# Table scatters in four spaced pairs per batch, each released by a cast, and a first plan a quarter later, in a gated attention and mixture-of-experts layer

## The chip, the cores and the metric

The kernel runs on one core of a Trainium2 chip. The metric is device time in microseconds (us) of one execution; lower is better. One execution was also taken by the hardware profiler, and every view below is of that one.

## The reference

The layer takes eight batches of 512 tokens with 256 features. Attention comes first: sixteen heads of sixteen features over a context, with a mask, and a gated sum into x. Then a normalised x goes through eight experts, of which each token uses its best two:

```python
logits = x_flat @ router_w + router_b
probs = jax.nn.softmax(logits, axis=-1)
top_w, top_idx = jax.lax.top_k(probs, TOP_K)
comb = jnp.sum(top_w[..., None] * jax.nn.one_hot(top_idx, E, dtype=x.dtype), axis=1)
output = jnp.zeros_like(x_flat)
for e in range(E):
    h = jax.nn.gelu(x_flat @ expert_up[e].T, approximate=False)
    out_e = h @ expert_down[e].T
    output = output + comb[:, e:e + 1] * out_e
```

The result is `x + tanh(g_ffn) * output`. The kernel computes only the two chosen experts of each token.

## The kernel before

**Two kinds of work share the engines.** A loop of passes (`for b in range(-1, B)` in `attend_near`) does attention for batch b, prepares batch b+1 and finishes older ones. Each pass has four groups g, and each group three places n; a slot is written (g, n). `between` fills a table `plan[g, n]` of steps, and the loop runs them in that order. The other kind of work is the expert jobs.

**Jobs.** Tokens are sorted by expert in groups of 256 rows (a pair of 128-row halves; four late jobs have one half). A job fetches its rows by an indirect gather (`fetch`, `xg`), turns them on TensorE (`turn`, `x_ps`), does the up product in four steps (`ups`, `h_ps`, line 622), GELU on ScalarE, the down product in two (`downs`, `o_ps`, line 640), adds the weighted result to rows `y` gathered from the output (`fetch_y`, line 594), and scatters them back (line 646). `load` brings an expert's two weight matrices, 1024 KB each, on SP's queue; their pool has three buffers. There are 36 jobs in the main list.

**The table.** Where a token goes is known after routing. `place` (GpSimd, lines 440 to 460) counts each token's place in its expert's list, leaves it in `at` and casts it to integers in `place_i`. `enter(t)` then scatters 128 tokens' entries to the `table` in DRAM, once for each of the two chosen experts: two indirect DMAs on GpSimd's queue (line 464), four calls a batch, eight scatters. `count` of `plan(k)` (VectorE, lines 506 to 556) works out, once a part of the batches is placed, which expert and which table line each job of that part has. `list_rows(s)` reads a job's lines of the table back to SBUF (`listed`) on SP's queue (line 576). The table is one DRAM tensor, so a list read waits for the scatters issued before it, and a later scatter waits for a list read issued before it.

**Order.** The framework's scheduler may issue an instruction earlier than its place in the program when its operands are ready sooner; a pinned instruction (`keep_in_program_order`) stays behind the instruction that the program put before it on the same engine. [...]The steps of a batch's placing run one pass after its routing: `place` at slot (0, 2), and `enter` at (0, 2), (1, 0), (1, 1), (1, 2), or, in a pass whose batch completes a part (b = 4 for the first part, b = 7 for the second), all at (0, 2) with `counts` behind.

**First jobs in the loop.** `amid` names, for (pass, group), the job steps that run among attention's: `begin` (the first list reads, gathers and loads) in (4, 3), the first up product in (5, 1), and jobs 0 to 3 complete by the end of pass 7. `DONE = 4` is the first job of the tail.

**The tail.** After the loop, `compute(s, MAIN, DONE)` gives each job's steps, eleven for a pair in the middle: the gather for job s+2, the y gather of s-1, four up steps, the turn of s+1, two down steps of s-1, the list read of s+3, the load of s+2. After each step one entry of `queue` runs: the last batch's remaining attention steps (`rest`), then places and entries of batches 6 and 7 with empty entries (`wait`) between them, then the last plans.

Of the kernel before, what the change touches and what calls it, by code (L numbers as in the profile page):

```python
# [24 lines left out]
QT = S // P  # L25
# [38 lines left out]
def flamingo_layer(ctx: ExitStack, tc: tile.TileContext, a: dict, out: bass.AP):  # L64
    nc = tc.nc
# [82 lines left out]
    place_i = fixed([P, B * QT, 2], "place_i", I32)  # L148
# [145 lines left out]
    def shared(p2, small, bank):  # L294
# [72 lines left out]
        def finish(b):  # L367

            x2T = p2.tile([P, DC, S], F32, tag="xnT", name=f"x2T{b}", bufs=1)
            said = {}  # L370
# [58 lines left out]
            def place():  # L429

                both = said["both"].rearrange("p t e -> p (t e)")
                ps = bank(f"place_ps{b}")
                n = QT * E
                nc.tensor.matmul(ps[:, :n], lhsT=before, rhs=both, start=True, stop=True)
                nc.tensor.matmul(ps[:, n : 2 * n], lhsT=ones, rhs=both, start=True, stop=True)
                counts = small.tile([P, 2, QT, E], F32, tag="counts", name=f"counts{b}", bufs=2)
                nc.scalar.copy(counts.rearrange("p i t e -> p (i t e)"), ps[:, : 2 * n])
                place = t3("place")
                for t in range(QT):
                    nc.gpsimd.tensor_tensor(place[:, t, :], counts[:, 0, t, :], filled, ALU.add)  # L440
                    nc.gpsimd.tensor_tensor(filled, counts[:, 1, t, :], filled, ALU.add)
                mine = slice(b * QT, (b + 1) * QT)
                at = small.tile([P, QT, 2], F32, tag="at", name=f"at{b}", bufs=2)
                picked = said["picks"]
                nc.gpsimd.tensor_tensor(
                    picked, picked, place.unsqueeze(2).to_broadcast([P, QT, 2, E]), ALU.mult
                )
                for k in (4, 2, 1):
                    nc.gpsimd.tensor_tensor(
                        at.unsqueeze(3) if k == 1 else picked[..., :k], picked[..., :k], picked[..., k : 2 * k],  # L450
                        ALU.add,
                    )
                entry = entries[:, b % 2]
                nc.gpsimd.tensor_copy(
                    entry[:, :, :, :2], tokens_i[:, mine].unsqueeze(2).unsqueeze(3).to_broadcast([P, QT, 2, 2])
                )
                nc.gpsimd.tensor_scalar(
                    entry.bitcast(F32)[:, :, :, 2], said["top"][:, :, :2], tg[:, 1:2], None, ALU.mult
                )
                nc.gpsimd.tensor_copy(place_i[:, mine, :], at)  # L460

            def enter(t):
                for i in range(2):
                    nc.gpsimd.indirect_dma_start(  # L464
                        out=table_parts[2 * t + i][:, :],
                        out_offset=bass.IndirectOffsetOnAxis(ap=place_i[:, t, i : i + 1], axis=0),
                        in_=entries[:, b % 2, t % QT, i, :], in_offset=None,
                    )
# [225 lines left out]
    def attend_near(att):  # L694
# [245 lines left out]
        def begin():  # L940
# [6 lines left out]
                list_rows(s)  # L947

        amid = {
            (4, 3): [lambda: None, lambda: None, begin],  # L950
            (5, 0): [lambda: None, lambda: None, lambda: turn_rows(0)],
            (5, 1): [lambda: fetch(2), lambda: fetch_y(0)] + ups(0),
            (5, 2): downs(0)[:1] + [lambda: load(2)],
            (5, 3): downs(0)[1:] + [lambda: turn_rows(1)],
            (6, 0): [lambda: fetch(3), lambda: fetch_y(1)] + ups(1),
            (6, 1): downs(1)[:1] + [lambda: load(3)],
            (6, 2): downs(1)[1:],
            (6, 3): [lambda: turn_rows(2)],
            (7, 0): [lambda: fetch(4), lambda: fetch_y(2)] + ups(2),
            (7, 1): downs(2) + [lambda: load(4), lambda: turn_rows(3)],  # L960
            (7, 2): [lambda: fetch_y(3)] + ups(3),
            (7, 3): [lambda: list_rows(5), lambda: list_rows(6), lambda: fetch(5)] + downs(3)
            + [lambda: load(5), lambda: turn_rows(4)],
        }
        DONE = 4


        xnT, later = {}, deque()
# [8 lines left out]
        for b in range(-1, B):  # L977
# [6 lines left out]
            plan = between(*(n if 0 <= n < B else None for n in (b - 1, b + 2, b + 3)))  # L984
            for place, enter, counts in behind_route:
                plan[0, 2].append(place)
                if counts:
                    plan[0, 2] += enter + counts
                else:
                    for where, step in zip(((0, 2), (1, 0), (1, 1), (1, 2)), enter):  # L990
                        plan[where].append(step)
            for g in range(4):
                c, i = g // 2, g % 2
                if b >= 0:
# [17 lines left out]
        rest = [step for steps in between(B - 1, None, None).values() for step in steps]  # L1012
        wait = lambda: None
        (place, enter, _), (last, enter_last, counts) = later
        mixed = [step for pair in zip(rest, [place, *enter] + [wait] * len(rest)) for step in pair]
        spread = [step for one in enter_last for step in (one, wait, wait)]
        queue = deque([*mixed, wait, last, *spread, *counts])
        for s in range(DONE, MAIN):
            for step in compute(s, MAIN, DONE):
                step()  # L1020
# [330 lines left out]
```

## Time and profile before

| what | us |
|---|---|
| runs, median of 3 | 853.23 (847.31 to 854.47) |
| the profiled execution | 875.95 |
| its span | 874.2 |
| last table scatter of batch 7 issued at | 476.36 |
| first up product of the first job at | 277.65 |

Times in a view count from the start of the span. PE is TensorE's matmuls, PEld its weight loads, DVE is VectorE, ACT ScalarE, POOL GpSimd, and SP the queue that issues the plain DMAs. The page cuts the span into 40 slices of 21.9 us and gives each engine's busy share in tenths; PEclk is the clock granted to TensorE, in tenths of full speed. A row of a timeline has its start, its length, engine, line, operation and operands, a count, and in brackets the engine's idle time before it and what ended it. A wait row has who waited for whom, the total, the number of waits and the longest.

### The profile page before, as it was taken

Reading aid. Unit: us, or ns where it says so; the run is one execution under the profiler, and the core shown is the slowest. Engines: PE = TensorE matmul, PEld = TensorE weight load, DVE = VectorE, ACT = ScalarE, POOL = GpSimd, SP = SyncE. Lnnn points to the kernel's source line nnn. Section 1 sums busy time; section 2 is a strip of 40 time slices with the busy share of each in tenths; the row PEclk is TensorE's granted clock in tenths of the full one; section 3 lists DMA queues with packets and bytes.
Section 4 is the critical chain, followed back from the end, with each engine's and each line's share of the span. In section 5 each row is a group of like instructions: output and inputs, shape, how many; then the busy total and the mean of one; then the engine's idle time right before and its main releaser. Section 6 shows DMA issues by size and latency. Waiting matters only on the chain. (4 is left out here: it accounts for less than half of the span.)

```text
span 874.2 us, 11291 instructions
## 1 busy us (share of the span) xinstructions
PE 797.5 (91%) x4090; PEld 579.2 (66%) x4090; DVE 315.8 (36%) x945; ACT 260.3 (30%) x501; POOL 319.4 (37%) x431
## 2 busy tenths in 40 slices
PE   1798999898799989999999699999999999999992
PEld 0353444343445566676878588888898898989881
DVE  5366778484868355653232011111110110111110
ACT  0444464445264523444331112111111111111210
POOL 5111105141345225164545443534333433434331
PEclk9778999696989999999999899999999999999997
DMA  4600011101066221315454857565667676667611
GB/s 140 244 7 7 7 49 33 49 26 50 2 211 215 81 79 57 116 31 189 136 158 137 296 157 244 177 228 184 213 190 246 197 240 198 209 222 241 211 49 35
DMA packets 86630, 121.59 MB, mean 139 GB/s; under 512 B 15693, under 2 KB 70368, under 8 KB 86560
## 3 DMA queue, kind: packets, MB, share of 16 engines
q1 hardware_dynamic: 74400, 93.68, 32.1%
q0 software_dynamic: 12160, 27.04, 10.1%
q8 instruction: 36, 0.59, 0.3%
q14 instruction: 34, 0.28, 0.1%
HBM read 101.05 MB, written 20.17 MB: 139 GB/s over the span
## 5 line engine op out<-in xcount | busy, mean ns | idle before, releaser
L640 PE MATMUL o_ps<-down,hT 128*128 128x256 f32 x1088 | 245.0, 383 | 7.2 <-DVE y L643 6.7
L622 PE MATMUL h_ps<-xT,up 128*128 128x256 f32 (+1 forms) x1152 | 245.3, 370 | 5.8 <-DVE oT L871 2.6
L622 PEld LDWEIGHTS h_ps<-xT,up 128*128 128x128 f32 x1152 | 209.5, 191 | 35.8 <-DVE oT L871 3.0
L640 PEld LDWEIGHTS o_ps<-down,hT 128*128 128x128 f32 x1088 | 205.9, 192 | 40.1 <-DVE y L643 7.2
L626 ACT ACTIVATE hT<-h_ps 128x512 f32<-128x512 f32 (+1 forms) x144 | 81.5, 573 | 364.7 <-PE h_ps L622 316.0
L643 DVE SCALAR_TENSOR_TENSOR y<-o_ps,listed,y 128x256 f32<-128x256 f32 x68 | 32.8, 484 | 280.1 <-DMA y<-out,listed 149.5
L594 POOL DMA_INDIRECT y<-out,listed x68 | 66.1, 971 | 157.0 <-DMA out<-y,listed 125.5
L646 POOL DMA_INDIRECT out<-y,listed x68 | 68.7, 1010 | 105.6 <-DVE y L643 76.6
L845 ACT ACTIVATE n_pT<-w_ps 128x512 f32<-128x512 f32 x128 | 71.0, 599 | 82.7 <-PE w_ps L841 58.6
L816 DVE TENSOR_REDUCE tops<-t_ps 128x4 f32<-128x512 f32 x128 | 79.4, 681 | 39.2 <-PE t_ps L812 39.0
L594 POOL DMA_INDIRECT xg<-rows,listed x68 | 64.8, 954 | 42.6 <-DMA listed<-table 17.7
L841 PE MATMUL w_ps<-ql,n_km 32*128 32x512 f32 x256 | 74.7, 714 | 3.5 <-DVE tops L816 2.5
L464 POOL DMA_INDIRECT table<-entries,place_i x64 | 62.4, 975 | 25.9 <-issue 16.5
L612 DVE COPY xT<-x_ps 128x512 f32<-128x512 f32 (+1 forms) x36 | 23.6, 655 | 98.9 <-PE x_ps L610 92.9
L812 PE MATMUL t_ps<-n_k,n_q 32*128 32x256 f32 x512 | 50.9, 429 | 2.7 <-ACT n_pT L845 1.8
L799 POOL TENSOR_TENSOR x<-x,bo 128x1024 f32<-128x1024 f32 x8 | 19.0, 2372 | 78.6 <-ACT xn_a L341 78.6
L812 PEld LDWEIGHTS t_ps<-n_k,n_q 32*128 32x128 f32 x512 | 29.8, 196 | 26.1 <-issue 13.4
L792 PE MATMUL q_ps<-n_xnT,wqT 128*128 128x512 f32 x64 | 36.7, 705 | 7.0 <-ACT n_q L796 6.9
L863 DVE STREAM_TRANSPOSE raw<-n_av 128x512 f32<-128x512 f32 x32 | 22.8, 713 | 51.6 <-PE n_av L858 40.4
L841 PEld LDWEIGHTS w_ps<-ql,n_km 32*128 32x128 f32 x256 | 23.7, 204 | 24.2 <-DVE tops L816 16.3
L858 PE MATMUL n_av<-n_pT,nv 128*32 128x512 f32 x256 | 39.5, 676 | 0.0
L878 PE MATMUL proj_ps<-woT,oT 128*128 128x256 f32 x128 | 32.9, 392 | 4.8 <-DVE oT L871 4.8
(208 smaller groups left out, 563.8 us busy)
## 6 DMA issues: line engine op xcount, KB each, us to landing
up<-in_upT SPq DMA_DIRECT2D x36, 1024.0 KB
down<-in_downT SPq DMA_DIRECT2D x36, 1024.0 KB
x<-in_x SPq DMA_DIRECT2D x8, 512.0 KB
out<-x SPq DMA_DIRECT2D x8, 512.0 KB
rows<-xn_f SPq DMA_DIRECT2D x8, 512.0 KB
table<-none SPq DMA_DIRECT2D x1, 2288.0 KB
xg<-rows,listed POOLq DMA_INDIRECT x68
y<-out,listed POOLq DMA_INDIRECT x68
```

Of the source, the lines that this page charges most:

```text
L464: nc.gpsimd.indirect_dma_start(out=table_parts[2 * t + i][:, :], out_offset=bass.IndirectOffsetOnAxis(ap=place_i[:, t, i : i + 1], axis=0) ...
L594: nc.gpsimd.indirect_dma_start(out=dst, out_offset=None, in_=src[: seen[JOBS[s][0]], :], in_offset=bass.IndirectOffsetOnAxis(ap=listed[:, ...
L622: nc.tensor.matmul(ps[:, i, :n], lhsT=up[:, dc, (f + i) * P : (f + i + 1) * P], rhs=xT[:, dc, :n], start=(dc == 0), stop=(dc == DC - 1),)
L626: nc.scalar.activation(made[s][:, f : f + 2, :n], ps[:, :, :n], AF.Gelu)
L640: nc.tensor.matmul(ps, lhsT=hT[:, f, h * P : (h + 1) * P], rhs=down[:, f, :], start=(f == 0), stop=(f == FC - 1))
L646: nc.gpsimd.indirect_dma_start(out=out_parts[h][:, :], out_offset=bass.IndirectOffsetOnAxis(ap=listed[:, n, h, 0:1], axis=0), in_=y[:, h, ...
L792: nc.tensor.matmul(ps, lhsT=w["wqT"][:, dc, c * P : (c + 1) * P], rhs=xnT[b][:, dc, :], start=(dc == 0), stop=(dc == DC - 1),)
L812: nc.tensor.matmul(ps[j][:, u], lhsT=q[rows_j, c, t * P : (t + 1) * P], rhs=k[rows_j, c], start=True, stop=True)
L816: nc.vector.tensor_reduce(top[:, 2 * tp : 2 * tp + 2, :].rearrange("p t (i x) -> p t i x", i=2)[:, :, :, 32 * j], ps[j], AX.X, ALU.max,)
L841: nc.tensor.matmul(ps[j], lhsT=km[rows_j, c, i, :], rhs=lowered[b, c][rows_j, i, :], start=True, stop=True)
L845: nc.scalar.activation(pT[:, j, :], ps[j], AF.Exp)
L858: nc.tensor.matmul(av[32 * j : 32 * j + 32, :], lhsT=made[b][3][:, 8 * c + 2 * j + r, :], rhs=pT[:, j, :], start=True, stop=True,)
```

## The change

The cast of the places moves from the end of `place` (one on GpSimd for a batch) into `enter` (one on VectorE for each call, pinned in program order), so that each pair of scatters has to wait for a VectorE instruction at a fixed place. The slots of the four calls become (1, 1), (2, 0), (2, 2), (3, 1), for every batch, and `counts` goes to (1, 2). `begin` goes to (5, 0), the first up product to (5, 3); jobs 0 to 2 are complete by the end of the loop, and `DONE` is 3. In the tail `rest` runs first without gaps, then each placing and entering step is followed by four empty entries.

```diff
-                nc.gpsimd.tensor_copy(place_i[:, mine, :], at)
+                said["at"] = at
 
             def enter(t):
+
+                tc.keep_in_program_order(nc.vector.tensor_copy(place_i[:, t, :], said["at"][:, t % QT, :]))
                 for i in range(2):
                     nc.gpsimd.indirect_dma_start(
...
         amid = {
-            (4, 3): [lambda: None, lambda: None, begin],
-            (5, 0): [lambda: None, lambda: None, lambda: turn_rows(0)],
-            (5, 1): [lambda: fetch(2), lambda: fetch_y(0)] + ups(0),
-            (5, 2): downs(0)[:1] + [lambda: load(2)],
-            (5, 3): downs(0)[1:] + [lambda: turn_rows(1)],
-            (6, 0): [lambda: fetch(3), lambda: fetch_y(1)] + ups(1),
-            (6, 1): downs(1)[:1] + [lambda: load(3)],
-            (6, 2): downs(1)[1:],
-            (6, 3): [lambda: turn_rows(2)],
-            (7, 0): [lambda: fetch(4), lambda: fetch_y(2)] + ups(2),
-            (7, 1): downs(2) + [lambda: load(4), lambda: turn_rows(3)],
-            (7, 2): [lambda: fetch_y(3)] + ups(3),
-            (7, 3): [lambda: list_rows(5), lambda: list_rows(6), lambda: fetch(5)] + downs(3)
-            + [lambda: load(5), lambda: turn_rows(4)],
+            (5, 0): [lambda: None, begin],
+            (5, 2): [lambda: turn_rows(0)],
+            (5, 3): [lambda: fetch(2), lambda: fetch_y(0)] + ups(0),
+            (6, 0): downs(0)[:1] + [lambda: load(2)],
+            (6, 1): downs(0)[1:] + [lambda: turn_rows(1)],
+            (6, 2): [lambda: fetch(3), lambda: fetch_y(1)] + ups(1),
+            (6, 3): downs(1)[:1] + [lambda: load(3)],
+            (7, 0): downs(1)[1:] + [lambda: turn_rows(2)],
+            (7, 1): [lambda: fetch(4), lambda: fetch_y(2)] + ups(2),
+            (7, 2): downs(2)[:1] + [lambda: load(4)],
+            (7, 3): downs(2)[1:] + [lambda: turn_rows(3), lambda: list_rows(5)],
         }
-        DONE = 4
+        DONE = 3
...
                 plan[0, 2].append(place)
-                if counts:
-                    plan[0, 2] += enter + counts
-                else:
-                    for where, step in zip(((0, 2), (1, 0), (1, 1), (1, 2)), enter):
-                        plan[where].append(step)
+                plan[1, 2] += counts
+                for where, step in zip(((1, 1), (2, 0), (2, 2), (3, 1)), enter):
+                    plan[where].append(step)
...
-        mixed = [step for pair in zip(rest, [place, *enter] + [wait] * len(rest)) for step in pair]
-        spread = [step for one in enter_last for step in (one, wait, wait)]
-        queue = deque([*mixed, wait, last, *spread, *counts])
+        queue = deque([*rest, place, wait, wait])
+        for step in (*enter, last, *enter_last):
+            queue.extend([step] + [wait] * 4)
+        queue.extend(counts)
```

## The prediction

> **What bounds the kernel now.** I read the page's busy shares and slices first, then the timeline of the matmuls for where each batch begins, then busy time by batch, and last the waits and timelines around the idle stretches. The chain that ended last is no help: it holds only the last scatter.
>
> ```profile
> PE 797.5 (91%) x4090; PEld 579.2 (66%) x4090; DVE 315.8 (36%) x945; ACT 260.3 (30%) x501; POOL 319.4 (37%) x431
> PE   1798999898799989999999699999999999999992
> PEclk9778999696989999999999899999999999999997
> ```
>
> TensorE is the bound, so time can come only from its idle slices and from slices at a low granted clock. There are three places: slices 8 and 10 (clock digit 6), slice 11 (7 busy), slice 23 (6 busy). The same by stage, each line from a batch's first weights matmul to the next one's (columns: length, busy time with counts, granted clock, DMA share, GB/s):
>
> ```profile
> 96.25:130.37 34.12, 32.48 (x210) 16.08 (x209) 26.46 (x66) 19.80 (x41) 2.34 (x1) 1.00 0.11 36
> 130.37:175.03 44.66, 40.69 (x214) 18.92 (x213) 29.84 (x88) 20.59 (x43) 13.50 (x24) 0.82 0.13 41
> 175.03:219.28 44.25, 40.86 (x214) 18.81 (x213) 28.85 (x86) 20.29 (x43) 13.63 (x24) 0.81 0.12 38
> 219.28:261.28 42.00, 36.76 (x214) 17.06 (x214) 31.96 (x101) 20.41 (x43) 19.13 (x30) 0.90 0.30 102
> 261.28:311.87 50.59, 48.08 (x287) 28.98 (x286) 29.23 (x82) 23.53 (x46) 19.23 (x30) 1.00 0.47 154
> 311.87:359.27 47.40, 44.41 (x259) 28.69 (x258) 27.59 (x81) 17.54 (x31) 17.13 (x29) 0.93 0.29 89
> 359.27:410.66 51.39, 49.82 (x265) 34.89 (x264) 24.38 (x91) 21.57 (x37) 22.84 (x35) 1.00 0.29 95
> 484.86:508.24 23.38, 16.66 (x67) 14.06 (x68) 1.96 (x4) 2.39 (x4) 10.55 (x11) 0.85 0.69 238
> 508.24:858.50 350.26, 349.49 (x1726) 309.04 (x1724) 39.67 (x75) 58.02 (x104) 139.18 (x143) 1.00 0.61 200
> ```
>
> The first line is pass b=1: attention, no scatter, no expert job, 34.1 us. Passes 2 and 3 do the same matmuls and take 10 us more; the only new work is the placing and eight scatters on GpSimd (2.34 to 13.5 us). Around the end of pass 2's eight:
>
> ```profile
> 154.67 0.96 POOL L464 DMA_INDIRECT table<-entries,place_i  x1 [0.30 <-issue]
> ...
> 157.12 0.72 DVE L863 STREAM_TRANSPOSE raw<-n_av 128x512 f32<-128x512 f32 x1 [3.77 <-remote]
> ...
> 157.95 2.70 PE L792 MATMUL q_ps<-n_xnT,wqT 128*128 128x512 f32 x4 [3.67 <-ACT n_q L796]
> ```
>
> The last scatter's issue ends at 155.6; VectorE, ScalarE and TensorE all stand until 157.1 and go on together, with no named releaser. Pass 3 repeats it (last scatter 198.92 + 0.96, TensorE idle 1.95 us). After each the clock is 0.50 for some 17 us. What holds the engines is not shown; the end of the burst is what both have in common. Passes 5 to 7 also have eight back to back and no such stop.
>
> The tail (508 to 858) is full. Before it, 484.86 to 508.24 holds one job's matmuls and takes 23.4 us; these are the waits from 478 to 500, then the SP queue's over the span (total, times, longest):
>
> ```profile
> DVE y L643 <- DMA y<-out,listed: 18.9, 1, 18.9
> PE o_ps L640 <- DVE y L643: 6.7, 1, 6.7
> POOL y L594 <- DMA out<-y,listed: 6.4, 1, 6.4
> POOL xg L594 <- DMA listed<-table: 3.9, 1, 3.9
> ...
> SPq L576 <- DMA table<-entries,place_i: 29.5, 4, 20.8
> ```
>
> The chain reads backwards: SP sits up to 20.8 us at a list read until the last batch's scatters have landed (its next read goes at 478.90, the last scatter at 476.36); three jobs' weight loads then leave in one burst, GpSimd's gather waits for its list, the scatter of y leaves late, the next y gather later, and VectorE can't free the PSUM bank.
>
> [...]one n_o multiply at 225.47 took 2.42 us, against a mean of 0.49, beside the 2.34 us bias add on GpSimd.
>
> **The change, part by part.**
>
> *Spacing, passes 2 and 3.* Without the stop they would take b=1's 34.1 us: (44.66 − 34.12) + (44.25 − 34.12) = 20.7 us. Bounds: 0, if something else holds the engines, to −20.7. In the profiled execution I take −18.
>
> *Spacing, pass 4.* 42.0 − 34.1 = 7.9 us, but the 3.07 us gap at 225 [...]before any scatter, and the plan's VectorE work stays. I take −2 (0 to −5).
>
> *Casts.* 8 GpSimd casts of 0.19 us go; 32 VectorE casts come, priced by the nearest row, the index cast of 128x32 at 181 ns: 5.8 us, 24 of them (4.3 us) inside the passes, where VectorE is busy 26 to 32 us a pass. I take +1.5 (0 to +4.3); in the tail VectorE is nearly idle.
>
> *The wait that a cast adds.* VectorE stands at a pinned cast until GpSimd has `at`; behind it are the maxima and transposes that TensorE waits for. `at` was done at 189.45 in pass 3 and 236.0 in pass 4; the statistics after which the cast is pinned ran from about 193 and 241.8. The margin is 4 to 6 us, so 0; it would pay if gathers hold GpSimd longer. On GpSimd, gathers and y scatters now stand behind a pair that waits for its slot; y is needed half a job (7 us) later, which hides it.
>
> *First plan, list reads and loads later.* `begin` moves from (4,3) to (5,0), first matmuls from (5,1) to (5,3). The four list and gather steps and 4 MB of loads (they ran from 250 to 266) keep more than two quarters, some 17 us. The plan's VectorE operations (234.9 to 238.4) move by a group; their reader is also later. 0.
>
> *One job moves into the tail.* A pair costs 13.9 us (starts of h_ps at 454.92 and 468.84). Inside the passes it costs the same: 50.59 − 13.9 = 36.7 and 47.40 − 13.9 = 33.5, against 34.1 without. Little idle time was being filled, so moving it is near neutral: +1 (0 to +4, with the now denser last steps of batch 7, whose VectorE and ScalarE chain of about 8.5 us may hold TensorE).
>
> *Tail spacing.* A pair every five steps, eleven steps a job, spreads eight pairs over four jobs; a list read waits for at most the two pairs just ahead, and the loads behind it have some 20 us until their job. The stop of 23.38 − 13.9 = 9.5 us goes, and 1.6 us ahead of it at 483. Late next is the y gather, which follows the y scatter by 6 to 7 us in every job and already fits. I take −9 (0 to −11).
>
> Sum on the profiled execution (875.95; span 874.2): −18 −2 +1.5 +1 −9 = −26.5, 849.5 us. The runs' median is 22.7 us shorter than the profiled one, about as much as the two stops cost, so they may be partly absent there; I halve that term to −9: 853.2 − 9 − 2 + 1.5 + 1 − 9 = 835.7. **Forecast 836.**
>
> **Rivals.**
> - *The stops of passes 2 and 3 are not the scatters'* (passes 5 to 7 have bursts without them) *or appear only under the profiler*, and the tail's stop goes only by half: 853.2 − 4.5 − 1 + 1.5 + 1 = 850.
> - *VectorE becomes hostage to GpSimd* (slower). In passes 5 to 7 gathers on GpSimd wait for transfers (y waits for out up to 7.6 us); if that delays `at` past the slot, VectorE stands, TensorE follows, and the clock halves. At 3 us each plus 3.4 us (a 6.8 us stretch at half clock) over three passes it is +19; with −9 from the tail and 2.5 of casts and moved job, 853.2 + 19 − 9 + 2.5 = 866. It decides once `at` is over 5 us later than before. Against it: the margins above.
> - *The casts don't hold the pairs*: VectorE runs ahead, pairs bunch as before: 853.2 + 2.5 = 856. In the tail VectorE does run ahead between its y updates, so two pairs may leave together.
>
> **How the numbers follow.** Forecast 0.55, not the scatters 0.22, hostage 0.15, no hold 0.08. The forecast's own range is 818 to 845: 853.2 − 20.7 − 5 − 11 + 1.5 = 818, and the upper end with the stops of passes 2 and 3 kept. For 8 in 10 I take 820 to 860, which leaves out most of the hostage case and the very bottom. About 1% is what a measurement here can tell from no change. Faster: nearly all of the forecast and a little of the second case, 0.57; same: the rest of it and most of the fourth, 0.25; slower 0.18.
>
> **What would show it.** Right: passes 2 and 3 near 35 us at clock 1.00; scatters as four separate pairs per pass; no 20 us wait of SP at line 576's read; no VectorE wait for o_ps-freeing y of 18.9 us. Wrong: VectorE waiting at its casts for `at`; clock 0.50 in new places of passes 5 to 7; idle TensorE at the start of the tail.

## The result, and the profile after

The changed kernel takes **859.72 us** (median of 16 runs, 851.17 to 863.5), the kernel before 852.91 (16 runs, 847.31 to 858.35): a ratio of **1.0065 [1.0037, 1.0093]** (the medians differ by 6.8 us, the means by 5.5). The brackets hold the 95% interval. Executions of a kernel over 1.5% above its fastest are left out of the medians and ratios. The forecast was 836, with 820 to 860 as its range. The profiled execution of after is 859.25 us long, its span 857.5; unlike that of before it agrees with its runs.

First the page of after, busy shares and the two rows of slices that were shown of before:

```profile
PE 784.6 (92%) x4090; PEld 573.8 (67%) x4090; DVE 315.7 (37%) x977; ACT 257.4 (30%) x499; POOL 317.1 (37%) x423
PE   1799999999999989798999989999999999999992
PEclk9897799999999989899999989999999999999997
```

The low digits of slices 8, 10 and 11 are gone. Low ones now stand at slices 15, 17, 19 and 24 (from 300, 343, 386 and 493 us): where jobs run among attention, and in the tail. The busy time by stage (length, then busy time of PE, PEld, DVE, ACT, POOL with counts, granted clock, DMA share, GB/s), passes 1 to 7 and then all that follows the last weights matmul:

```profile
93.45:130.80 37.35, 35.72 (x210) 17.07 (x210) 25.94 (x65) 19.69 (x41) 2.35 (x1) 0.88 0.10 33
130.80:166.19 35.39, 33.46 (x214) 16.27 (x213) 28.71 (x89) 20.14 (x43) 11.19 (x20) 1.00 0.16 51
166.19:201.69 35.50, 33.41 (x214) 16.28 (x213) 28.77 (x90) 20.14 (x43) 13.23 (x23) 1.00 0.15 47
201.69:239.23 37.54, 35.24 (x215) 16.72 (x214) 30.94 (x107) 20.31 (x43) 13.18 (x23) 0.95 0.09 31
239.23:282.82 43.59, 41.16 (x250) 22.53 (x249) 30.63 (x86) 21.85 (x45) 25.14 (x36) 1.00 0.60 202
282.82:332.87 50.05, 46.33 (x275) 30.54 (x274) 26.83 (x82) 19.08 (x33) 15.93 (x26) 0.93 0.32 104
332.87:371.78 38.91, 33.48 (x152) 21.15 (x152) 20.00 (x85) 13.52 (x24) 10.05 (x21) 0.87 0.20 65
371.78:857.50 485.72, 461.28 (x2286) 403.44 (x2278) 71.18 (x214) 86.65 (x153) 206.70 (x233) 0.98 0.57 186
```

Passes 2, 3 and 4 did what was forecast: 35.4, 35.5 and 37.5 us at a clock near 1, against 44.7, 44.3 and 42.0. The stage lines also say what the stops had cost. Pass 2 became 9.3 us shorter; its matmuls' busy time fell by 7.2 us (40.69 to 33.46), TensorE's idle time only by 2.0 (3.97 to 1.93). So most of the loss was the half clock after the stop, 16.0 us of pass 2 before and none after, and not the standing itself. Some standing there is ordinary: in pass 1, without any scatter, TensorE is idle for 1.28 us at the same matmul.

Passes 5 to 7 last 132.6 us against 135.3, although a job of 13.9 us has left them; pass 7 has a clock of 0.87 and TensorE idle for 5.4 us. What follows the last weights matmul takes 485.7 us against 477.7.

Against the profiled execution of before the account is −22.5 in passes 2 to 4, −2.7 in passes 5 to 7 and +8.0 behind them. Against its *runs* the changed kernel is 6.8 us longer. The profiled execution of before was 23 us longer than its runs, about what its stops in passes 2 and 3 cost. This suggests that the runs compared did not have these stops; the experiments come back to it.

Three places in after show what came in. In pass 7 (rows of the timeline, left-out rows between them):

```profile
346.16 1.00 POOL L596 DMA_INDIRECT y<-out,listed  x1 [4.54 <-DMA out<-y,listed]
...
348.43 0.23 POOL L440 TENSOR_TENSOR place<-counts,filled 128x8 f32<-128x8 f32 x1
...
350.64 0.27 DVE L508 SCALAR_TENSOR_TENSOR count<-iota_e,filled 128x8 f32<-128x8 f32 x1 [7.44 <-POOL filled L441]
...
357.03 0.14 DVE L464 CAST place_i<-at 128x2 int32<-128x2 f32 x1
...
360.06 1.09 ACT L341 ACTIVATE xn_f<-x,shift_f,rstd_end_f 128x256 f32<-128x256 f32 x2 [8.12 <-DVE shift_f L330]
361.05 0.57 ACT L628 ACTIVATE hT<-h_ps 128x512 f32<-128x512 f32 x1
...
361.68 3.04 PE L843 MATMUL w_ps<-ql,n_km 32*128 32x512 f32 x4 [5.43 <-ACT hT L628]
```

Read it forwards: GpSimd stands 4.5 us until a y scatter has landed, then gathers job 2's y; batch 5's placing, whose counts were there at 344.16, is queued behind that and starts at 348.43. VectorE stands 7.4 us at the second part's plan (line 508), which needs `filled`; its statistics come behind the plan; ScalarE stands 8.1 us at the normalisation that needs these; job 2's GELU is queued behind that, keeps its PSUM banks, and TensorE stands 5.4 us until ScalarE has emptied one. Half clock goes with it for 10.2 us (358.5 to 368.7). The cast, done at 357.03, waited for nothing of its own.

In pass 6 TensorE stands from 308.55 to 312.27, while VectorE works without a pause. In the tail it stands from 492.07 to 495.73, as before, but for less; these are the waits from 485 to 500 us, and then SP's at the list reads over the span (total, times, longest):

```profile
DVE y L645 <- DMA up<-in_upT: 15.0, 1, 15.0
...
POOL y L596 <- DMA out<-y,listed: 6.4, 1, 6.4
...
PE o_ps L642 <- DVE y L645: 3.7, 1, 3.7
```

```profile
SPq L578 <- DMA table<-entries,place_i: 99.3, 14, 19.1
```

VectorE's 15 us are put down to a weight load, but what it needs is y, whose gather left only at 488.96, after 6.4 us of waiting for the y scatter. SP stood 29.5 us in 4 list read waits before. Five of the 14 waits now (13.4 us) lie in passes 4 and 5, the other nine behind them.

### The profile page after: what moved, and what is told of

It is laid out like the page before. It is cut to its first block, busy times and chain, and to the rows that moved or that the text cites. A ratio compares the mean times of both kernels' runs of the same rounds, so it can differ in the third digit from the quotient of the medians.

```text
span 857.5 us, 11308 instructions
## 1 busy us (share of the span) xinstructions
PE 784.6 (92%) x4090; PEld 573.8 (67%) x4090; DVE 315.7 (37%) x977; ACT 257.4 (30%) x499; POOL 317.1 (37%) x423
## 5 line engine op out<-in xcount | busy, mean ns | idle before, releaser
L466 POOL DMA_INDIRECT table<-entries,place_i x64 | 62.5, 977 | 76.2 <-DVE place_i L464 35.1
L814 PE MATMUL t_ps<-n_k,n_q 32*128 32x256 f32 x512 | 44.3, 404 | 2.0 <-ACT n_pT L847 1.2
L814 PEld LDWEIGHTS t_ps<-n_k,n_q 32*128 32x128 f32 x512 | 26.5, 185 | 23.4 <-issue 13.8
L794 PE MATMUL q_ps<-n_xnT,wqT 128*128 128x512 f32 x64 | 33.8, 654 | 5.7 <-ACT n_q L798 5.1
L860 PE MATMUL n_av<-n_pT,nv 128*32 128x512 f32 x256 | 37.5, 651 | 0.0
```

The costliest lines, as they stand in the source:

```text
L466: nc.gpsimd.indirect_dma_start(out=table_parts[2 * t + i][:, :], out_offset=bass.IndirectOffsetOnAxis(ap=place_i[:, t, i : i + 1], axis=0) ...
L794: nc.tensor.matmul(ps, lhsT=w["wqT"][:, dc, c * P : (c + 1) * P], rhs=xnT[b][:, dc, :], start=(dc == 0), stop=(dc == DC - 1),)
L814: nc.tensor.matmul(ps[j][:, u], lhsT=q[rows_j, c, t * P : (t + 1) * P], rhs=k[rows_j, c], start=True, stop=True)
L860: nc.tensor.matmul(av[32 * j : 32 * j + 32, :], lhsT=made[b][3][:, 8 * c + 2 * j + r, :], rhs=pT[:, j, :], start=True, stop=True,)
```

## The experiments

The kernels ran on several chips, told here by number. Each is compared with runs of the kernel before on the same chip. That took 875.1 us on chip 8, 874.8 on chip 10, 870.5 on chip 5, 867.4 on chip 15 and 852.0 on chip 7. Each chip was used in one session only, so "chip" below may as well mean the session. For the comparison above (852.9) the chip isn't known. The first expectations give times for a chip where the kernel before takes about 853 us; on the other chips the ratio is what counts.

### Are the stops real, and where does the gain lie?

*before_again*: the kernel before, once more (chip 8).

> The kernel before, unchanged, profiled a second time. If the stops of passes 2 and 3 belong to that one profiled execution, these passes take 35 to 36 us each at a granted clock of 1.00 and the span is near 851 us; if every burst of eight scatters holds the engines, they take 44 us again and the span is near 874.

Measured: 877.16 us; passes 2 and 3 take 42.4 and 39.1 us with TensorE idle for 2.0 us at 155.6, pass 5 takes 55.5, and the tail's stop is there (492.64, 6.2 us). So the stops aren't an accident of one profiled execution. Nor do they come after every run of scatters: TensorE stands 3.0, 2.0 and 2.3 us at the ends of those of passes 4, 5 and 7, and not after the eight of pass 6, which end at 344. The prediction's remark that passes 5 to 7 have no such stop holds for the first profile only.

*passes_only*: the kernel before with casts and spaced pairs in passes 2, 3, 5 and 6 alone (batches 0, 1, 3 and 4).

```diff
+                said["at"] = at
+                if b not in (0, 1, 3, 4):
+                    nc.gpsimd.tensor_copy(place_i[:, mine, :], at)
...
+                if b in (0, 1, 3, 4):
+                    tc.keep_in_program_order(nc.vector.tensor_copy(place_i[:, t, :], said["at"][:, t % QT, :]))
...
-                    for where, step in zip(((0, 2), (1, 0), (1, 1), (1, 2)), enter):
+                    for where, step in zip(((1, 1), (2, 0), (2, 2), (3, 1)), enter):
```

> The kernel before with the casts and the four spaced slots in passes 2, 3, 5 and 6 alone; the passes with a plan, the job slots and the tail stay. If the loss comes from the casts on VectorE, 2 to 5 us slower than before (855 to 858). If it comes from the moved job steps in pass 7, no change (852 to 854). The prediction's first term would make it 9 us faster (844).

*tail_only*: the kernel before with casts for batches 6 and 7 and the changed kernel's tail queue.

> The kernel before with the new tail alone: the last batch's attention steps without gaps, then each placing and entering step followed by four empty entries, with pinned casts for batches 6 and 7. By the prediction's tail term 9 us faster (844); by the trace of the changed kernel, where the stop near 492 only shrank, about 3 us faster (850); if the casts cost in the tail, slower than 853.

*uncast*: the changed kernel with one GpSimd cast for a batch again and no pins.

```diff
-                said["at"] = at
+                nc.gpsimd.tensor_copy(place_i[:, mine, :], at)
...
-                tc.keep_in_program_order(nc.vector.tensor_copy(place_i[:, t, :], said["at"][:, t % QT, :]))
```

> The changed kernel with one cast for a batch on GpSimd at the end of the placing, as before, and no pinned cast; all slots, the plan's slot, the job steps and the tail's order stay as changed. If the moved job steps of pass 7 are what costs, it stays at 857 to 861. If the pinned casts cost, it comes back to 853 or below.

| chip 8 | us | ratio to before | passes 2, 3 | passes 5 to 7 | behind them |
|---|---|---|---|---|---|
| before_again | 877.2 | | 42.4, 39.1 | 142.0 | 478.4 |
| passes_only | 856.7 | 0.9797 [0.9744, 0.9849] | 35.4, 35.5 | 134.8 | 476.5 |
| tail_only | 873.3 | 0.9993 [0.9961, 1.0024] | 43.3, 39.1 | 143.7 | 475.7 |
| uncast | 879.1 | 1.0068 [1.0039, 1.0097] | 42.3, 39.1 | 142.3 | 482.1 |

Spacing in the passes is worth 2% here, more than any of the three expectations had; the tail's spacing is worth nothing that can be told from zero, where 9 or 3 us were expected. Without the casts the slots alone hold nothing: the scatters bunch again, the stops return, and a stop of 5.8 us in pass 7 is there without any cast.

*pool_gaps* (chip 10): the kernel before, slots and cast as they were, with memsets of a 128x256 tile on GpSimd among the scatters of passes 2 and 3.

```diff
+                if b < 2 and t % QT:
+                    for _ in range(6):
+                        tc.keep_in_program_order(nc.gpsimd.memset(filler, 0.0))
                 for i in range(2):
```

> The kernel before with GpSimd memsets put among the scatters of passes 2 and 3, so that they no longer follow each other at 1.26 us; no cast, no other slot. If it is the density of the burst that holds the engines, the stops of passes 2 and 3 shrink or go and the time falls by up to 12 us where the kernel before has them. If only the slots matter, it stays level.

Measured: 863.69 us, 0.9881 [0.9816, 0.9946]. Its passes 2 and 3, in the columns used above:

```profile
125.65:161.15 35.50, 33.46 (x215) 16.28 (x214) 28.96 (x86) 20.15 (x43) 19.25 (x42) 1.00 0.16 51
161.15:196.93 35.78, 33.41 (x215) 16.28 (x214) 28.76 (x86) 20.12 (x43) 19.17 (x42) 1.00 0.15 47
```

The eight scatters still go in one burst, but 1.45 us apart from start to start instead of 1.28, since a memset of 0.3 us stands between two. For these two passes that is as good as spacing the pairs over half a pass: what mattered in them was the unbroken run, not the slot. TensorE still stands 1.4 and 1.7 us at the end of the bursts, at full clock.

### Does the changed kernel lose the gain where the stops are?

*after_again* (chip 10): the changed kernel, unchanged.

> The changed kernel, unchanged, on the chip that this job is given. If the kernel before has the stops of passes 2 to 4 here (875 us), the spacing pays here and the changed kernel stands near 860, 15 us faster; if the kernel before is at 853 here, the changed one is again 5 to 7 us slower.

*spaced_all*: the kernel before with casts and spaced pairs in passes 2, 3, 5 and 6 and the new tail; the job steps, the plans and the bursts of passes 4 and 7 where they were. The edit is shown against passes_only.

```diff
-                if b not in (0, 1, 3, 4):
+                if b not in (0, 1, 3, 4, 6, 7):
...
-        mixed = [step for pair in zip(rest, [place, *enter] + [wait] * len(rest)) for step in pair]
-        spread = [step for one in enter_last for step in (one, wait, wait)]
-        queue = deque([*mixed, wait, last, *spread, *counts])
+        queue = deque([*rest, place, wait, wait])
+        for step in (*enter, last, *enter_last):
+            queue.extend([step] + [wait] * 4)
+        queue.extend(counts)
```

> The kernel before with pinned casts and the four spaced slots in passes 2, 3, 5 and 6 and with the new tail, but with the old job steps, the old plan slot and the old bursts in passes 4 and 7. If the moved job steps of pass 7 are what the changed kernel loses by, this beats the changed kernel by 5 to 10 us (850 to 855 where that one is at 860). If the tail or the casts are what it loses by, it stands level with the changed kernel or above.

*place_first*: the changed kernel with job 4's gather and job 2's y gather pinned behind batch 5's placing in pass 7.

```diff
-                nc.gpsimd.tensor_copy(
+                copied = nc.gpsimd.tensor_copy(
...
+                if b == 5:
+                    tc.keep_in_program_order(copied)
...
+            if (s == 4 and src is rows) or (s == 2 and src is out):
+                tc.keep_in_program_order(ins)
```

> The changed kernel with the row gather of job 4 and the y gather of job 2 pinned behind the placing in pass 7 on GpSimd. If the stop near 356 comes from the placing waiting behind that y gather, VectorE's wait at the plan falls from 7.4 to 2 to 3 us, TensorE's 5.4 us gap and the half clock behind it go, and the time falls by 5 to 10 us against the changed kernel. If the stop comes from ScalarE's order alone or from the y scatter ahead of both, nothing changes.

| chip 10 | us | ratio to before | passes 2, 3 | passes 5, 6, 7 | behind them |
|---|---|---|---|---|---|
| after_again | 872.65 | 0.9977 [0.9950, 1.0004] | 35.4, 35.5 | 51.0, 50.3, 39.1 | 489.5 |
| place_first | 867.21 | 0.9925 [0.9898, 0.9952] | 35.4, 35.4 | 51.0, 50.2, 35.3 | 490.7 |
| spaced_all | 853.58 | 0.9772 [0.9718, 0.9826] | 35.4, 35.5 | 49.4, 47.5, 38.7 | 473.9 |

On a chip that has the stops, all three remove them from passes 2 and 3; the changed kernel is still no faster than the kernel before, where after_again was expected to gain 15 us. What it has over spaced_all costs 19 us: the later plans, the job steps that follow them, the pairs of passes 4 and 7 and the moved job. Placing before gathering brings back 5.4 us. Of this the profiles show 3.9 in pass 7, where VectorE's wait at the plan is 3.25 us and TensorE's stop falls from 5.6 to 1.4; behind the passes nothing is gained. So the chain read above is a cause, and not the whole.

Pass 5 shows another. In after_again ten indirect DMAs follow each other without a pause, from 266.05 on, since both gathers had to wait for their list:

```profile
266.05 0.99 POOL L596 DMA_INDIRECT xg<-rows,listed  x1 [3.73 <-DMA listed<-table]
...
277.61 0.97 POOL L466 DMA_INDIRECT table<-entries,place_i  x1 [0.30 <-issue]
...
280.43 0.58 ACT L352 COPY x2T<-xnT_ps_f 128x512 f32<-128x512 f32 x1 [2.22 <-remote]
280.57 2.48 DVE L818 TENSOR_REDUCE tops<-t_ps 128x4 f32<-128x512 f32 x4 [4.38 <-remote]
281.32 2.07 PE L624 MATMUL h_ps<-xT,up 128*128 128x256 f32 x4 [5.35 <-DVE tops L818]
```

ScalarE, VectorE and TensorE go on within 1 us of each other, 2 us after the last issue, with no named releaser; TensorE stood 5.35 us. The first profile of the same kernel has the same run, two scatters longer (263.98 to 279.06), and there the engines go on through it:

```profile
275.50 0.68 DVE L818 TENSOR_REDUCE tops<-t_ps 128x4 f32<-128x512 f32 x1
275.54 0.97 POOL L466 DMA_INDIRECT table<-entries,place_i  x1 [0.30 <-issue]
275.63 2.54 PE L624 MATMUL h_ps<-xT,up 128*128 128x256 f32 x11
...
278.10 0.96 POOL L466 DMA_INDIRECT table<-entries,place_i  x1 [0.30 <-issue]
278.10 0.64 PE L389 MATMUL route_ps<-x2T,rw 128*32 128x128 f32 x16
```

One program, one run of DMAs, a stop in one profile and none in the other (pass 5: 51.0 and 43.6 us). after_third and job_kept below repeat the two outcomes on chips 5 and 7. What holds the engines is shown by no view.

### Do pauses help the changed kernel?

*after_gaps* (chip 5): the changed kernel with one memset ahead of each table scatter of batches 3 to 5.

```diff
                 for i in range(2):
+                    if b in (3, 4, 5):
+                        tc.keep_in_program_order(nc.gpsimd.memset(filler, 0.0))
```

> The changed kernel with one memset of a 128x256 tile on GpSimd (0.3 us) ahead of each of the 24 table scatters of batches 3, 4 and 5 (passes 5, 6 and 7); GpSimd's order is otherwise the changed kernel's. Theory A (a run of some ten indirect DMAs without a pause holds up what the other engines report): the stops near 276 us (5.35 in the last profile of the changed kernel) and near 391 us (6.06), each at the end of such a run, shrink to under 2 us and lose their half clock; the stops of passes 6 and 7 near 318 and 366 us stay (3.7 and 5.6), as they follow y's gather and the plan; the time is 8 to 12 us under the changed kernel's on the same chip. If this chip shows no stop at the end of such runs (as the first profile of the changed kernel showed none near 276), the time is the changed kernel's within 2 us. Theory B (the moved job steps' order alone makes the stops): all four stay and the time is the changed kernel's or 1 to 3 us more, on either chip.

*after_third*: the changed kernel on the same chip.

> The changed kernel once more, as the measure for the run with pauses on the same chip. Theory A: where the kernel before takes about 875 us here, 871 to 874 with stops near 276 and 391 us; where the kernel before takes about 853, 858 to 861 with no stop near 276. Theory B: 6 to 7 us more than the kernel before, on either chip.

*before_gaps*: the kernel before with the memset ahead of all 64 table scatters.

> The kernel before, its order kept, with one memset of a 128x256 tile on GpSimd ahead of each of its 64 table scatters, in all passes and the tail. Theory A: as with the pauses in passes 2 and 3 alone (a ratio of 0.9881), and the stops of passes 4 and 5 at the ends of scatter runs go as well (2 to 4 us each with their half clock): a ratio of 0.975 to 0.982 on a chip where the kernel before takes about 875, and within 0.5% of 1 on one where it takes about 853. The stop of the tail (6 us, at an o_ps) stays, since its scatters already stood apart. Theory B (only the slots matter and the pauses' gain in passes 2 and 3 was theirs by chance): a ratio of 0.988 at best, with stops in passes 4 and 5 as before.

*spaced_gaps*: spaced_all with the memset ahead of all 64.

> The best kernel so far (the kernel before with casts and four spaced pairs in passes 2, 3, 5 and 6 and the new tail, the job steps where they were) with the same memset ahead of each of the 64 table scatters, which splits up the bursts that were left in passes 4 and 7. Theory A: the stops left there near 291 and 361 us (3.1 and 2.4) shrink or go, the tail's (4.2) may; a ratio of 0.968 to 0.975 on a chip where the kernel before takes about 875, and 0.99 to 1.0 on one where it takes about 853. Theory B: the ratio without the memsets (0.977), or up to 0.003 above it for what the memsets cost.

| chip 5 | us | ratio to before | passes 5, 6, 7 | behind them |
|---|---|---|---|---|
| after_third | 870.54 | 1.0001 [0.9974, 1.0028] | 50.9, 50.4, 38.8 | 489.2 |
| after_gaps | 863.41 | 0.9929 [0.9900, 0.9957] | 47.2, 48.8, 38.2 | 485.1 |
| before_gaps | 858.58 | 0.9867 [0.9816, 0.9918] | 50.3, 47.3, 37.3 | 478.9 |
| spaced_gaps | 860.81 | 0.9892 [0.9848, 0.9936] | 49.4, 47.4, 37.1 | 480.5 |

Pauses alone bring the changed kernel 7.1 us, a little under what was expected: the stop of pass 5 shrinks from 5.0 to 2.8 us only (the gathers in that run had no pause), and the stop of 3.8 us at 390 goes, though one of 2.2 us at an x_ps follows. before_gaps came out above its expected band (0.975 to 0.982), and no run shows why: the stops of passes 4 and 5 went as expected, and the tail's stop of 6.3 us stayed as expected. spaced_gaps missed too (0.968 to 0.975): its ratio is above the 0.9772 that spaced_all had on chip 10, and its tail has two stops, of 6.0 and 4.5 us. Spaced_all wasn't run on chip 5, so what the memsets did to it isn't known.

### The later plan or the moved job?

*job_moved*: spaced_all with job 3 left to the tail; the plan where it was.

```diff
-            (7, 2): [lambda: fetch_y(3)] + ups(3),
-            (7, 3): [lambda: list_rows(5), lambda: list_rows(6), lambda: fetch(5)] + downs(3)
-            + [lambda: load(5), lambda: turn_rows(4)],
+            (7, 3): [lambda: list_rows(5)],
         }
-        DONE = 4
+        DONE = 3
```

> The kernel with the pairs spaced and cast and the job steps where they were (0.9772 of the kernel before), with one thing more: job 3's up, gather of y and down steps leave pass 7 for the tail (DONE = 3), the first plan staying where it was. There the passes 5 to 7 took 135.6 us and what follows the last pass 473.9; in the changed kernel on the same chip 140.4 and 489.5. Theory L (the later first plan is what costs: it brings list, gathers and scatters together in passes 5 to 7): passes 5 to 7 give up the job, 122 to 126 us, the tail takes it, 485 to 488, and the ratio stays 0.975 to 0.982. Theory J (moving a job into the tail is what costs, since in the passes it filled time that was idle): passes 5 to 7 stay at 132 to 136, the tail takes 485 to 488, and the ratio is 0.988 to 0.995.

*job_kept*: the changed kernel with its later plan, but jobs 1 to 3 closed up so that four are done before the tail.

```diff
-            (6, 3): downs(1)[:1] + [lambda: load(3)],
-            (7, 0): downs(1)[1:] + [lambda: turn_rows(2)],
-            (7, 1): [lambda: fetch(4), lambda: fetch_y(2)] + ups(2),
-            (7, 2): downs(2)[:1] + [lambda: load(4)],
-            (7, 3): downs(2)[1:] + [lambda: turn_rows(3), lambda: list_rows(5)],
+            (6, 3): downs(1) + [lambda: load(3), lambda: turn_rows(2)],
+            (7, 0): [lambda: fetch(4), lambda: fetch_y(2)] + ups(2),
+            (7, 1): downs(2) + [lambda: load(4), lambda: turn_rows(3)],
+            (7, 2): [lambda: fetch_y(3)] + ups(3),
+            (7, 3): [lambda: list_rows(5), lambda: list_rows(6), lambda: fetch(5)] + downs(3)
+            + [lambda: load(5), lambda: turn_rows(4)],
         }
-        DONE = 3
+        DONE = 4
```

> The changed kernel, all its casts and spaced pairs and its later first plan kept, but with jobs 1 to 3 closed up in passes 6 and 7 so that four jobs are done before the tail, as in the kernel before (DONE = 4). Theory L: passes 5 to 7 take the changed kernel's 140 and the job's 12 on top, 149 to 154 us, the tail 474 to 479, and the ratio stays near the changed kernel's, 0.993 to 1.003. Theory J: passes 5 to 7 take 138 to 144, the tail 474 to 479, and the ratio is 0.982 to 0.988.

*mended*: the changed kernel with the edits of after_gaps and place_first together.

> The changed kernel with both single repairs at once: the memsets ahead of the scatters of batches 3, 4 and 5 (which took 7 us off) and the placing of batch 5 ahead of the two gathers in pass 7 (which took 5 us off). If the two stops are separate, the gains add: a ratio of 0.985 to 0.989, with passes 5, 6 and 7 near 47, 49 and 35 us. If one stop only moved to another place, the better of the two is left: 0.991 to 0.994.

*spaced_again*: spaced_all as it was, on the same chip.

> The best kernel so far, unchanged, as the measure for the others on the same chip: 0.977 of the kernel before where that takes about 875 us, passes 2 and 3 at 35.4 and 35.5 us, passes 5 to 7 at 135 to 136 and 474 to 480 after them. On a chip where the kernel before takes about 853: 0.99 to 1.0.

| chip 7 | us | ratio to before | passes 5, 6, 7 | behind them | pass 5 to the end |
|---|---|---|---|---|---|
| spaced_again (neither) | 847.51 | 0.9945 [0.9925, 0.9964] | 49.4, 46.5, 36.9 | 473.6 | 606.5 |
| job_kept (later plans) | 848.71 | 0.9962 [0.9942, 0.9982] | 43.6, 54.4, 36.8 | 473.6 | 608.4 |
| job_moved (moved job) | 844.58 | 0.9919 [0.9891, 0.9947] | 49.4, 46.5, 29.5 | 478.7 | 604.1 |
| mended (both) | 853.86 | 1.0025 [1.0000, 1.0050] | 43.1, 49.0, 32.2 | 487.8 | 612.1 |
| *the first after (both, not mended)* | *859.72* | *1.0065 [1.0037, 1.0093]* | *43.6, 50.0, 38.9* | *485.7* | *618.3* |

The last row is from the first comparison, where the kernel before took 852.9. "Later plans" stands for a bundle: both plans and the first jobs' steps later, and the pairs of passes 4 and 7 cast and spaced. These weren't tried one by one. Taken alone, the bundle costs 1.4 us (0.9962 − 0.9945, of 852) and the moved job gains 2.2 us; neither is certain to differ from nothing. Together they cost 6.8 us even when mended, and some 10 us unmended by the first comparison. So neither theory as it was put (L or J alone) holds: Theory L wanted 149 to 154 us in job_kept's passes 5 to 7, where 134.8 was measured, and Theory J 132 to 136 in job_moved's, where it was 125.4.

The stage lines of job_moved and of mended, passes 5 to 7 together and then what follows, show where the two part:

```profile
238.19:363.58 125.39, 119.95 (x695) 77.44 (x694) 75.35 (x241) 52.33 (x97) 49.43 (x82) 0.97 0.31 100
363.58:842.24 478.66, 457.92 (x2261) 399.25 (x2258) 73.07 (x219) 88.37 (x157) 201.12 (x227) 0.98 0.58 191
```

```profile
240.48:364.82 124.34, 116.91 (x674) 72.27 (x674) 76.87 (x252) 54.39 (x101) 57.15 (x101) 0.99 0.41 133
364.82:852.60 487.78, 462.67 (x2286) 404.77 (x2278) 71.71 (x214) 86.65 (x153) 210.30 (x239) 0.98 0.57 185
```

Mended has 21 matmuls fewer in the passes, but is only 1 us shorter there; behind them it has 25 more (4.75 us of busy time) and takes 9.1 us more. The rest, 4.4 us, is idle time: TensorE stands 2.8 us at 384.5 for a gather's rows, and 3.9 us at 489 for y. Its pass 7 shows that the placing came earlier:

```profile
346.22 0.27 DVE L515 SCALAR_TENSOR_TENSOR count<-iota_e,filled 128x8 f32<-128x8 f32 x1 [3.25 <-POOL filled L442]
...
350.61 0.95 POOL L603 DMA_INDIRECT y<-out,listed  x1 [0.30 <-issue]
...
357.60 2.09 PE L852 MATMUL w_ps<-ql,n_km 32*128 32x512 f32 x4 [1.58 <-ACT hT L637]
```

The plan waited 3.25 us instead of 7.44, the y gather goes behind, TensorE's stop is 1.58 us instead of 5.43, and pass 7 took 32.2 us instead of 38.9. The expected ratio was missed; it was put for a chip with stops, where the two repairs brought 7.1 and 5.4 us one at a time. Here, with no stop in pass 5 to remove, 1.0025 stands against the 1.0065 of the first comparison. That is 3.4 us, but the two intervals overlap and the comparisons were made apart, so it isn't certain that the repairs gain anything here.

### Does the kernel before stop where it takes 852 us?

*before_third*: the kernel before, once more (chip 15).

> The kernel before, unchanged, for its trace. Chips 5, 8 and 10 ran it in 873 to 875 us, chip 7 in 852. Theory A (the stops at the ends of scatter runs belong to some chips only): on a chip that takes about 852 the passes 2, 3, 4 and 5 last 35.4, 35.5, 39 to 40 and 44 to 50 us with no stop over 1.5 us in passes 2 and 3; on one that takes about 875 they last 42 and 39 and 44 and 55 with the stops, as seen. Theory B (the stops are on every chip, and the faster chips save their time elsewhere): stops of 2 to 4 us in passes 2 and 3 on either.

*job_moved_again*: the fastest kernel, on the same chip (15).

> The fastest kernel so far (pairs cast and spaced in passes 2, 3, 5, 6 and the tail, the first plan where it was, one job moved into the tail; 0.9919 where the kernel before takes 852), unchanged. Where the kernel before takes about 875 Theory A expects 0.970 to 0.978, since the stops of passes 2, 3 and 5 go there too, and Theory B about 0.99; where it takes about 852 both expect 0.989 to 0.995.

The kernel before took 867.42 us here, so this was another chip with stops, where both theories expect them: this run doesn't decide between the two. before_third's passes 2 and 3:

```profile
125.91:168.09 42.18, 38.16 (x215) 17.63 (x214) 28.63 (x86) 20.58 (x43) 13.56 (x24) 0.88 0.13 43
168.09:207.09 39.00, 35.76 (x215) 16.92 (x214) 28.69 (x86) 20.18 (x43) 13.55 (x24) 0.96 0.14 43
```

job_moved_again took 850.89 us, a ratio of 0.9786 [0.9721, 0.9852]. So this kernel is faster than the kernel before on both kinds of chip; the changed kernel itself ran on neither 7 nor 15.

The kernel before was never profiled on a chip where it takes 852 us. That it has no stops there is inferred, from these things:

- The changed kernel's run of indirect DMAs has no stop in the first comparison, nor has that of job_kept on chip 7.
- Two kernels were profiled on both kinds of chip, and both leave the run of eight in pass 7 as it was. TensorE stands 2.4 us at its end in spaced_all (chip 10) and 2.2 us in job_moved_again (chip 15), and at most 0.7 us in spaced_again and job_moved (chip 7). Pass 7 took 38.7 and 31.6 us against 36.9 and 29.5. This alone is no proof, since before_third has no stop of 1.5 us there either.
- The kernel before had a mean granted clock of 0.954 to 0.957 (medians over its runs) on chips 5, 8, 10 and 15, and 0.965 on chip 7. On chip 10 spaced_all, without most of the stops, had 0.965.
- spaced_all is worth 2.3% on chip 10 and 0.55% on chip 7, and its times on the two, 853.6 and 847.5 us, are far closer than those of the kernel before, 874.8 and 852.0.

## Why the prediction was wrong, step by step

- **Spacing, passes 2 and 3 (−18 in the profiled execution, halved to −9).** Mechanism right, and the size right for the profile: 18.0 us went (88.9 to 70.9 for the two). *The halving failed.* What the term is worth depends on the chip: −18 for the profile shown, −10 to −11 on chips 8 and 15 (81.5 and 81.2 us before), and, as inferred above, next to nothing where the comparison ran. There −9 was forecast. The 22.7 us between the profiled execution and its median was the sign of this; I took half of it. On chips 8 and 15 half would have been right, by luck. The first rival (stops that the runs don't have) was the better reading here.
- **Spacing, pass 4 (−2).** 42.0 became 37.5 in the first profile; on chips 5 and 10 it is 39.1, against 43.7 and 43.4 before on chips 8 and 15. Little of this is pass 4's own spacing: with its burst left as it was, it takes 42.1 us in passes_only, 40.4 in spaced_all and 39.2 in spaced_again. So −2 is of the right size where the stops are, and where they aren't the term is next to nothing (39.1 in job_kept). The gap of 3.07 us, which the forecast had stay, ends at 228.69 in the first profile of before, ahead of the pass's first scatter (236.59). It isn't in the first profile of the changed kernel, where TensorE's longest gap in pass 4 is 1.55 us; the last section shows the multiply ahead of it.
- **Casts (+1.5), and the wait that a cast adds (0).** Right or lower: with casts passes 2 and 3 take 35.4 and 35.5 us, with memsets and no cast 35.5 and 35.8. No cast held VectorE in pass 7. GpSimd waited 35.1 us (14 times) for casts, and no stop of TensorE is traced to that. In pass 6, where VectorE works without a pause, the stop is 2.6 us before, 3.1 with casts (passes_only) and 3.7 in the changed kernel, so casts may have a small part in it.
- **First plan later (0) and one job moved into the tail (+1).** *This step failed*, as a sum: +1 forecast, 7 to 10 us measured. Each is nearly right alone (+1.4 and −2.2 us, neither certain to differ from nothing). The step that was wrong is to put the slots' change at nothing because the plan's reader moves as well. Together the job steps stand in other groups of passes 6 and 7; a y gather that waits for its scatter comes ahead of batch 5's placing, and behind that the plan, the statistics, the GELU and TensorE. The hostage rival named this chain, GpSimd held by y and VectorE held by GpSimd, with the wrong link: it is the plan that waits, not the cast. The 6.8 us at half clock that this rival puts behind each stop are the length of two such stretches of before (from 240.9 and 496.9); the stop in pass 7 of the changed kernel goes with 10.2. I read the margin of `at` in passes 3 and 4, where no gathers hold GpSimd ahead of it. place_first shows this part (5.4 us where the stops are; mended, 3.4, agrees without being clear of noise); the waits for gathered rows and y at the tail's start are argued from mended's profile. How they would fall with the slots moved again wasn't tried.
- **Tail spacing (−9).** *Failed.* tail_only gives 0.9993, with 475.7 us behind the passes against 478.4. "A list read waits for at most the two pairs just ahead" didn't free the tail: in tail_only SP stood 43.3 us in 4 such waits, in before_again on the same chip 36.6 in 4, and in the changed kernel 99.3 in 14. There the loads behind them still bunched (five loads and three list reads from 475 to 487 us), and the y gather landed late: 3.7 us of the stop stayed, with half clock for 6.8 us (from 494.9). That the bunched loads delay y is argued from their order, not tested. SP's waits alone don't set the time: job_moved, the fastest kernel, has 83.2 us of them.

The sum can be split at spaced_again on chip 7, if the first comparison was on a chip like it. That kernel has the spacings of passes 2, 3, 5 and 6 and the tail with their casts, put at −9, −9 and +1.5, and gained 4.5 us: 12 us are missing there. What the changed kernel has beyond it was put at −1 (−2, 0 and +1) and cost some 10: another 11. Together that is the 23 to 24 us between the forecast and the measurement.

## What to carry to other kernels

When a profiled execution is 2% longer than its runs, find out which of its stops the runs have before pricing any of them: a stop that isn't in the runs can't be gained there. Two steps that are each free when moved alone can cost when moved together, so check a moved step in the slots that it gets: what is queued ahead of it on GpSimd, and which engine's queue stands behind it. Where a run of indirect DMAs must stay, a short instruction between two of them is a cheap cure to try (1.2% on chip 10, 1.3% on chip 5, no gain shown where the pairs were spaced already).

## What the runs showed of the hardware

- On chips 5, 8, 10 and 15, at the end of many runs of eight to ten indirect DMAs on GpSimd, about 1.28 us apart from start to start, VectorE, ScalarE and TensorE stood for 2 to 5 us and went on together some 1.5 to 3 us after the last issue. Other such runs had no stop (before_again: pass 6, and the eleven that end at 478). At 1.45 us apart, with a memset of 0.3 us between, the half clock of passes 2 and 3 was gone. In the first comparison and on chip 7 a run of twelve had no such stop. What holds the engines, and what differs between these chips or sessions, isn't known.
- Half clock came behind gaps of TensorE of different lengths, some under 2 us. In before_third TensorE stood for 1.96 us (193.27 to 195.23), and the clock is 0.50 for 3.4 us from 195.4. In the first profile of before it is 0.50 for 17.1 us both from 159.0 and from 203.4, behind gaps of 3.67 us (to 157.95) and 1.95 us (to 202.26). Behind the gap of 3.07 us that ends at 228.69 it stays at 1.00 until 240.9. So the gap's length alone didn't decide.
- One `n_o` multiply on VectorE is long in each of the two first profiles: 2.42 us in before (from 225.47) and 1.77 us in the changed kernel (from 253.11). The other 31 of each took 0.42 to 0.47 us. Each starts inside a bias add of `x` on GpSimd (225.27 to 227.61 and 252.23 to 254.59) and ends 0.3 us after it. Behind the first of them TensorE stood the 3.07 us. Why they are long is not shown by any view.
- The start of pass 2 falls anywhere from 125.4 to 134 us in these profiles, in stages that no edit here touches. It goes with early half clock: 13.7 us of it ahead of pass 2 in spaced_all (125.4), 27.3 in the first profile of before (130.4), 34.1 in tail_only (134). Spans are therefore compared from pass 5 on in the last table.
